# Graph stack, first attention layer: output sums divided by row sums before they are turned, the inverse taken through DRAM

## The chip, the cores and the metric

One core of one Trainium2 chip runs the whole program. The metric is device time in microseconds (us), lower is better. TensorE is called PE here, VectorE DVE, ScalarE ACT, GpSimd POOL and SyncE SP; PEld is PE's weight load. An engine works through its instructions in program order, so an instruction that waits holds up those behind it; SP computes nothing here and only issues DMAs.

## What is computed

Four layers on 4096 nodes with 256 features, each of the form `x = layernorm(x + layer(x, adj))`. The change touches the first layer alone, a graph attention with four heads of 64 features:

```
Wh = (h @ W).reshape(n, heads, d)
s_i = einsum('nhd,hd->nh', Wh, a[:, :d]);  s_j = einsum('nhd,hd->nh', Wh, a[:, d:])
e = leaky_relu(s_i[:, None, :] + s_j[None, :, :], 0.2)
e = where((adj == 0)[:, :, None], -inf, e)
alpha = softmax(e, axis=1)
out = einsum('ijh,jhd->ihd', alpha, Wh).reshape(n, heads * d)
return elu(out)
```

The softmax's division is done last: for each node and head a weighted sum of 64 features and one row sum are added up, and the sum is divided by the row sum.

## The kernel before

The first layer is `additive_heads`. The 4096 target nodes are cut into NB = 8 blocks b of QW = 512, the source nodes into NT = 32 tiles j of P = 128. For each (b, j):

- SP loads the mask, two tiles j at a time (L306), into one of four buffers ("mask", 512 KB).
- ACT makes the factors of one tile from `row` and `dst`, four instructions of 128x512 (L313; L311 in the tiles called APART, j = 3, 11, 19, 27), into one of seven buffers ("prob").
- DVE masks them: one instruction of 128x2048 (L328), in APART tiles four of 128x512 (L319).
- PE adds them up in `sums` (L338): for each of the four heads two matmuls for the 64 features and, outside APART, one for the row sum, into `acc[b]`, three PSUM banks: two with features, the third with row sums. The weights are 32 columns wide, and a head's results lie in its own 32 partitions. In the trace each such matmul is two records. In APART tiles POOL's DMA (L323, L325) collects the probabilities in `den` in place of the third matmul, and at the block's end four matmuls over `den` (L342) close the row sums.

PE stands in the order of the code, two units behind the weights (LAG = 2); in all other engines' streams a scheduler places the instructions. `masked`, `factors` and the like are handles of instructions, and `issue_after(handle)` orders an instruction behind another of the same engine without a semaphore.

When block b is summed, ACT copies one bank and DVE two of them to SBUF (`kept`, L346), and the block is finished in pieces while block b+1 runs (`finish`, called with the j of block b+1):

- j = 4 and 10: `turned` (L353): two groups of nodes at a time, three transposes each (two of features, one of row sums) into a PSUM bank "g". At j = 4, `rows(b + 2)` also puts one transpose of source terms (L292) into such a bank; ACT copies it to `line` (L294), SP writes it to DRAM in four DMAs ("far", L297) and reads it back to all partitions ("row", L299, 1 MB).
- j = 4, 7, 10, 13: `outputs` for one group each: reciprocal of four row sums per node (L358), division (L360), and the positive part of the result added to X (L232).
- j = 11, 14, 17, 20: `add_exponential` for one group each: ACT's exponential (L238), its part below 1 added to X on DVE (L239), and the statistics of the layernorm (L156, L157).
- j = 22 to 30: the root of variance plus EPS (L182 on DVE, L161 and L162 on ACT, L168 to L171 on DVE) and the scaling of the four groups (L186).

The last block (b = 7) is finished in `tail`, in the opening of the second layer. The pools that matter: "ga_z" (prob) 7 buffers, "ga_mask" 4, "ga_ps" (banks "g") 2, "ga_pa" (acc) 2, "ga_o" (the tile `o`) 4.

Of the kernel before, what the change touches and what calls it, by code (L numbers as in the profile page):

```python
# [9 lines left out]
FP = mybir.dt.float32  # L10
# [3 lines left out]
AF = mybir.ActivationFunctionType  # L14
OP = mybir.AluOpType
# [13 lines left out]
def kernel(  # L29
# [32 lines left out]
    def pool(stack, name, bufs, **kw):  # L62
        return stack.enter_context(tc.tile_pool(name=name, bufs=bufs, reuse_waits="tile", **kw))
# [5 lines left out]

    ident = const.tile([P, P], FP, name="ident")  # L70
    make_identity(nc, ident)
    ones = const.tile([P, P], FP, name="ones")
    nc.vector.memset(ones, 1.0)

# [21 lines left out]
    def spread(pl, ap, dims, shape, name, eng):  # L96

        sb = pl.tile(shape, FP, name=name)
        eng.dma_start(sb, bass.AP(tensor=ap.tensor, offset=ap.offset, ap=[[0, P]] + dims))
        return sb  # L100
# [53 lines left out]
    def one_row(mv, k, y):  # L154
        st = fin.tile([P, 6], FP, name="bn")
        nc.vector.bn_stats(st, y)  # L156
        nc.vector.bn_aggr(mv[:, k, :], st)  # L157
# [7 lines left out]
    def end_root(v, r, n, eng=nc.vector):  # L165

        s = fin.tile([P, n], FP, name=f"s{n}")
        eng.tensor_tensor(s, r, r, OP.mult)  # L168
        eng.tensor_tensor(s, s, v, OP.mult)
        eng.tensor_scalar(s, s, -0.5, 1.5, OP.mult, OP.add)  # L170
        eng.tensor_tensor(r, r, s, OP.mult)  # L171
# [7 lines left out]
    def begin_root(mv):  # L179
        n = mv.shape[1]  # L180
        v = fin.tile([P, n], FP, name=f"v{n}")
        nc.vector.tensor_scalar_add(v, mv[:, :, 1], EPS)  # L182
        return v, first_root(v, n), n

    def scale_row(y, mv, r, k):
        nc.vector.tensor_scalar(y, y, mv[:, k, 0:1], r[:, k:k + 1], OP.subtract, OP.mult)  # L186

# [46 lines left out]
    def add_exponential(o, b, k, mv, seen=None):  # L234

        y = X[:, b * QB + k, :D]
        with tc.issue_after(getattr(seen, "ins", seen)) if seen is not None else nullcontext():
            nc.scalar.activation(o, o, AF.Exp)  # L238
        nc.vector.scalar_tensor_tensor(y, o, 1.0, y, OP.min, OP.add)  # L239
        one_row(mv, k, y)  # L240

    def additive_heads(a, H, slope, early, narrow, ahead):
# [9 lines left out]
        with ExitStack() as lay:  # L252
# [10 lines left out]
            rp = pool(lay, "ga_row", 2)  # L263
            zp = pool(lay, "ga_z", 7)
            sb = pool(lay, "ga_sb", 2)
            op = pool(lay, "ga_o", 4)
            mp = pool(lay, "ga_mask", 4)
            dp = pool(lay, "ga_den", 1)
            dr = pool(lay, "ga_dram", 2, space=bass.MemoryType.DRAM)
# [5 lines left out]
            def bank():  # L275
                return ps.tile([P, QW], FP, name="g")
# [13 lines left out]
            def rows(b, pr):  # L290

                nc.tensor.transpose(pr[:QB * H, :P], src[:, b * QB:(b + 1) * QB, :].rearrange("p k h -> p (k h)"), ident)  # L292
                line = sb.tile([QB * H, P], FP, name="line")
                nc.scalar.copy(line, pr[:QB * H, :P])  # L294
                far = dr.tile([H, QB, P], FP, name="far")
                for k in range(QB):
                    nc.sync.dma_start(far[:, k, :], line[k * H:(k + 1) * H, :])  # L297
                row[b] = rp.tile([P, H, QW], FP, name="row")
                nc.sync.dma_start(row[b].rearrange("p h i -> p (h i)"),  # L299
                                  far.rearrange("h k i -> (h k i)").unsqueeze(0).to_broadcast([P, H * QW]))  # L300

            def weights(b, j, rows=None):
                m = b, j // MJ
                if j % MJ == 0:
                    mask[m] = mp.tile([P, MJ, QW], I32, name="mask")
                    nc.sync.dma_start(mask[m], edges[:, j:j + MJ, b * QW:(b + 1) * QW])  # L306
                z = prob[b, j] = zp.tile([P, H, QW], FP, name="prob")
                for h in range(H):
                    r = rows[h] if rows else row[b][:, h, :]
                    if j in APART:  # L310
                        seen = nc.scalar.mul(z[:, h, :], r, dst[:, j, h:h + 1])  # L311
                    else:
                        seen = nc.scalar.activation(z[:, h, :], r, AF.Relu, bias=-1.0, scale=dst[:, j, h:h + 1])  # L313
                factors[b, j] = seen
                if rows:
                    keep_rows(rows)
                if j in APART:
                    for h in range(H):
                        nc.vector.scalar_tensor_tensor(z[:, h, :], z[:, h, :], V[:, j, D + h:D + h + 1],  # L319
                                                       mask[m][:, j % MJ, :], OP.max, OP.mult)  # L320
                    if j == APART[0]:
                        den[b] = dp.tile([P, H, QW], FP, name="den")
                        seen = nc.gpsimd.dma_start(den[b], z)  # L323
                    else:
                        seen = nc.gpsimd.dma_start(den[b], z, accum_op=OP.add)  # L325
                    narrow(seen)
                    return
                nc.vector.scalar_tensor_tensor(z, z, 1.0, mask[m][:, j % MJ, :].unsqueeze(1).to_broadcast([P, H, QW]),  # L328
                                               OP.add, OP.mult)

            def sums(b, j):
                if j == 0:
                    acc[b] = pa.tile([P, HC + 1, QW], FP, name="acc")
                for n in range(HC if j in APART else HC + 1):
                    for h in range(H):
                        lo = h * d + n * G
                        part = V[:, j, lo:lo + G] if n < HC else V[:, j, D + h:D + h + 1].to_broadcast([P, G])
                        nc.tensor.matmul(acc[b][h * G:(h + 1) * G, n, :], part, prob[b, j][:, h, :],  # L338
                                         start=(j == 0), stop=(j == NT - 1 and n < HC))
                if j == NT - 1:  # L340
                    for h in range(H):
                        nc.tensor.matmul(acc[b][h * G:(h + 1) * G, HC, :], ones[:, :G], den[b][:, h, :],  # L342
                                         start=False, stop=True)
                    kept[b] = [fin1.tile([P, QW], FP, name=f"kept{c}") for c in range(HC + 1)]
                    for c in range(HC + 1):
                        (nc.vector.tensor_copy if c else nc.scalar.copy)(kept[b][c], acc[b][:, c, :])  # L346
                    mvs[b] = fin.tile([P, QB, 2], FP, name="mv")

            def turned(bank, b, k):

                po = bank().rearrange("p (c f) -> p c f", f=P)
                for c in range(HC + 1):
                    nc.tensor.transpose(po[:, c, :], kept[b][c][:, k * P:(k + 1) * P], ident)  # L353
                return po

            def outputs(sb, po, b, k):
                rden = fin.tile([P, H], FP, name="rden")
                nc.vector.reciprocal(rden, po[:, HC, ::G])  # L358
                o = out[b, k] = sb.tile([P, D], FP, name="o")
                nc.vector.tensor_tensor(o.rearrange("p (h c e) -> p h c e", h=H, c=HC),  # L360
                                        po[:, :HC, :].rearrange("p c (h e) -> p h c e", h=H),
                                        rden.unsqueeze(2).unsqueeze(3).to_broadcast([P, H, HC, G]), OP.mult)
                add_positive(o, b, k)

            def finish(b, j):

                if j in (4, 10):
                    k = (j - 4) // 3
                    pos[b, k], pos[b, k + 1] = turned(bank, b, k), turned(bank, b, k + 1)
                    if k == 0 and b + 2 < NB:  # L370
                        rows(b + 2, pos[b, 0][:, HC + 1, :])
                if j in (4, 7, 10, 13):
                    k = (j - 4) // 3
                    outputs(op, pos[b, k], b, k)
                if j in (11, 14, 17, 20):
                    k = (j - 11) // 3
                    add_exponential(out[b, k], b, k, mvs[b], factors[b + 1, j + LAG])
                elif j == 22:
                    roots[b] = begin_root(mvs[b])
                elif j == 24:  # L380
                    end_root(*roots[b])
                elif j in (25, 27, 28, 30):
                    k = (25, 27, 28, 30).index(j)
                    scale_row(X[:, b * QB + k, :D], mvs[b], roots[b][1], k)

            def turn(b, bank=bank):
                if b + 2 < NB:
# [6 lines left out]
                groups = [(0, HC + 1, side), (HC + 1, 1, bank().rearrange("p (n f) -> p n f", n=1))]  # L394
                additive_values(xTs[b], b, groups, w_sb, V, src, dst, H, slope, APART)

            pos, roots, xTs, out, factors = {}, {}, {}, {}, {}
            LAG = 2
            units = [(b, j) for b in range(NB) for j in range(NT)]
            with tc.manual_schedule(engines={mybir.EngineType.PE}):  # L400
# [1057 lines left out]
```

## Time and profile before

| | |
|---|---|
| median of 3 runs | 2767.89 us (2765.59 to 2771.09) |
| the profiled execution's own time | 2767.82 us |
| its span | 2766.0 us |
| PE busy over the span | 2750.1 us (99%) |
| DVE | 2311.0 us (84%) |
| ACT | 1696.6 us (61%) |
| POOL | 1075.5 us (39%) |
| granted PE clock in 100 to 700 us | 1.00 |

The profile is of one execution; its span starts with the first instruction and ends with the last. The first layer's sums run from about 20 us to 703 us. A line of a timeline gives start, duration, engine, source line, operation, output and inputs, and how many instructions were put together; in brackets stands the idle time of the engine before it and what ended it. Durations of neighbours overlap a little, so the distance from start to start is what one costs. "L338" is line 338 of the kernel before.

### The profile page before, as it was taken

How to read it: one execution, taken by the hardware profiler on the slowest of the kernel's cores; microseconds unless marked ns; L12 is line 12 of the kernel's file. 1: busy time of each engine (PE TensorE's matmuls, PEld its weight loads, DVE VectorE, ACT ScalarE, POOL GpSimd, SP SyncE). 2: the span in 40 equal slices, each digit the busy share in tenths (PEclk: the TensorE clock that was granted, in tenths of full speed). 3: DMA queues.
4: the chain of work that ended last, by engine and by line, in shares of the span. 5: the costliest groups of instructions: out<-in, count | busy, mean ns of one | idle time of the engine just before them, and what ended most of it. 6: DMA issues, size and time to landing. Idle time of an engine off the chain costs nothing. (4 is left out here: it accounts for less than half of the span.)

```text
span 2766.0 us, 50161 instructions
## 1 busy us (share of the span) xinstructions
PE 2750.1 (99%) x19365; PEld 1444.9 (52%) x19365; DVE 2311.0 (84%) x3121; ACT 1696.6 (61%) x2660; POOL 1075.5 (39%) x1020
## 2 busy tenths in 40 slices
PE   9999999999999999999999999999999999999999
PEld 5333333333543333333333336888888777777776
DVE  8899999999777788887888888888888876677776
ACT  8899999999346666666666665565655422222222
POOL 0000000000049878878788786454455000000000
PEclk9999999999999999999999999999999999999999
DMA  8798998987449899898998988577778544454442
GB/s 236 150 191 189 194 196 191 189 188 168 97 117 191 180 190 187 189 190 183 194 187 186 193 178 208 155 203 212 190 197 236 108 76 76 77 81 80 76 70 45
DMA packets 279673, 445.48 MB, mean 161 GB/s; under 512 B 55321, under 2 KB 156169, under 8 KB 274442
## 3 DMA queue, kind: packets, MB, share of 16 engines
q0 software_dynamic: 108784, 216.29, 46.9%
q1 hardware_dynamic: 164280, 218.88, 26.8%
q10 hardware_dynamic: 6370, 7.10, 0.8%
q8 instruction: 152, 2.49, 0.4%
q14 instruction: 87, 0.71, 0.1%
HBM read 335.94 MB, written 39.40 MB: 136 GB/s over the span
## 5 line engine op out<-in xcount | busy, mean ns | idle before, releaser
L888 DVE TENSOR_TENSOR prob<-p,mask 128x1024 f32<-128x1024 f32 x512 | 619.3, 1222 | 162.7 <-ACT p L878 157.0
L878 ACT ACTIVATE p<-p,shift 128x1024 f32<-128x1024 f32 x512 | 555.6, 1088 | 319.7 <-PE p L876 319.1
L338 PE MATMUL acc<-prob,V 128*32 128x512 f32 x5888 | 638.1, 593 | 1.2 <-DVE prob L328 1.1
L898 POOL TENSOR_TENSOR den<-den,prob 128x1024 f32<-128x1024 f32 x220 | 557.6, 2534 | 89.8 <-DVE prob L888 87.1
L313 ACT ACTIVATE prob<-row,dst 128x512 f32<-128x512 f32 x892 | 557.9, 711 | 3.3 <-PE acc L338 2.8
L876 PE MATMUL p<-qT,kT 64*64 64x512 f32 x4096 | 531.5, 591 | 2.3 <-DVE prob L888 2.3
L912 PE MATMUL acc<-prob,V 64*64 64x512 f32 x4096 | 530.1, 589 | 0.0
L328 DVE SCALAR_TENSOR_TENSOR prob<-prob,mask 128x2048 f32<-128x2048 f32 x224 | 507.4, 2285 | 12.6 <-ACT prob L313 11.7
L338 PEld LDWEIGHTS acc<-prob,V 128*32 128x32 f32 x5888 | 189.1, 110 | 434.1 <-issue 407.2
L484 PE MATMUL acc<-mix,mixed 128*128 128x256 f32 x1476 | 401.4, 380 | 1.9 <-DVE quarters L506 1.0
L912 PEld LDWEIGHTS acc<-prob,V 64*64 64x64 f32 x4096 | 157.6, 133 | 281.9 <-issue 280.1
L484 PEld LDWEIGHTS acc<-mix,mixed 128*128 128x128 f32 x1476 | 279.1, 190 | 45.3 <-PE acc L484 3.1
L876 PEld LDWEIGHTS p<-qT,kT 64*64 64x64 f32 x4096 | 154.4, 133 | 279.3 <-issue 252.1
L1185 DVE TENSOR_TENSOR prob<-prob,mask 128x1024 f32<-128x1024 f32 x128 | 156.4, 1222 | 142.9 <-ACT prob L1176 142.9
L904 POOL DMA_DIRECT2D den<-prob x240 | 233.5, 973 | 63.7 <-DMA den<-prob 34.1
L484 PE MATMUL acc<-prob,X 128*128 128x256 f32 x984 | 252.9, 380 | 0.6 <-ACT quarters L498 0.6
L1104 POOL DMA_DIRECT2D mask<-in_adjT x64 | 47.6, 744 | 529.1 <-DVE prob L1185 510.3
L484 PEld LDWEIGHTS acc<-prob,X 128*128 128x128 f32 x984 | 186.8, 190 | 79.8 <-issue 59.2
L617 DVE SCALAR_TENSOR_TENSOR prob<-r,own,mask 128x512 f32<-128x512 f32 x252 | 177.0, 743 | 48.1 <-POOL mix L476 11.9
L1176 ACT ACTIVATE prob<-p 128x512 f32<-128x512 f32 x144 | 86.1, 598 | 212.5 <-PE p L1172 212.5
L325 POOL DMA_DIRECT2D den<-prob x24 | 21.1, 878 | 475.7 <-DVE prob L319 475.7
L1176 ACT ACTIVATE prob<-g 128x512 f32<-128x512 f32 x112 | 66.9, 597 | 199.3 <-PE g L1172 199.3
(245 smaller groups left out, 3044.7 us busy)
## 6 DMA issues: line engine op xcount, KB each, us to landing
mask<-in_adjT SPq DMA_DIRECT2D x254, 512.0 KB
den<-prob POOLq DMA_DIRECT2D x240, 512.0 KB, 5.4
den<-prob POOLq DMA_DIRECT2D x32, 1024.0 KB, 9.2
mask<-edges SPq DMA_DIRECT2D x512, 64.0 KB
mask<-in_adjT POOLq DMA_DIRECT2D x64, 512.0 KB, 5.7
edges<-in_adj POOLq DMA_DIRECT2D x32, 512.0 KB, 17.1
far<-squares SPq DMA_DIRECT2D x16, 512.0 KB
den<-prob SPq DMA_DIRECT2D x16, 512.0 KB
```

Of the source, the lines that this page charges most:

```text
L313: seen = nc.scalar.activation(z[:, h, :], r, AF.Relu, bias=-1.0, scale=dst[:, j, h:h + 1])
L328: nc.vector.scalar_tensor_tensor(z, z, 1.0, mask[m][:, j % MJ, :].unsqueeze(1).to_broadcast([P, H, QW]), OP.add, OP.mult)
L338: nc.tensor.matmul(acc[b][h * G:(h + 1) * G, n, :], part, prob[b, j][:, h, :], start=(j == 0), stop=(j == NT - 1 and n < HC))
L484: nc.tensor.matmul(acc[at][:, half * HW:(half + 1) * HW], w, a, start=(g == 0 and n in (0, 2, 3, 5)), stop=(g == NP - 1), skip_group_check ...
L617: nc.vector.scalar_tensor_tensor(z[:, n, :], r, ga.own[:, j:j + 1], mask[:, n, :], OP.add, OP.mult)
L876: nc.tensor.matmul(p[c * d:(c + 1) * d, r, :], kT[half, c, at:at + d], qT[half, c, cols], start=True, stop=True)
L878: nc.scalar.activation(p, p, AF.Exp, bias=shift)
L888: nc.vector.tensor_tensor(z, p, mask[m][:, j % MJ, :].unsqueeze(1).to_broadcast([P, KC, QW]), OP.mult)
L898: nc.gpsimd.tensor_tensor(to, to, flat, OP.add)
L904: nc.gpsimd.dma_start(to, flat, accum_op=OP.add)
L912: nc.tensor.matmul(acc[b][c][r * d:(r + 1) * d, :], V[half, j, r * d:(r + 1) * d], prob[b, j][half, r, :], start=(j == 0), stop=(j == NH - 1))
L1185: nc.vector.tensor_tensor(z, z, co.mask[b, 2 * g // MJ][:, lo:lo + 2, :], OP.mult)
```

## The change

In the changed kernel, for the blocks 0 to 6, the features are divided while nodes still lie along the free axis, and turned afterwards:

- Only the row sums are copied at the end of a block, by ACT. Seven DMAs on SP's queue and one instruction make their inverse: `there` (four rows of 512 to DRAM), `few` (back as 128 x 16, so that a reciprocal costs 16 elements per partition), a reciprocal on DVE bound behind the masking of tile 9 of block b+1, `back` (to DRAM), and `rden` (four DMAs, each one row spread to 32 partitions).
- DVE multiplies the two feature banks in PSUM by `rden`, bound behind the masking of tile 14 of block b+1, in place of the copies. `acc[b]` is held until then.
- PE turns two groups at a time, at j = 14 and 16, with four transposes each and no row sums; the transposes write their bank in four runs of 32 columns. The transpose of `rows` stays at j = 4, alone, in a bank of its own.
- Positive part and exponential work on two groups in one instruction (128 x 512) and read PSUM.
- The mask load of tile 16 is ordered behind the last `rden` DMA on SP.
- The root takes EPS as ACT's bias, from a constant tile that POOL sets, and three DVE instructions replace five.
- "ga_o" has one buffer of each of its tiles in place of four.

For block 7 the three copies stay: ACT now makes two of them and DVE one. In the order of the built programs the engines' streams behind the first layer are the same.

```diff
+    eps = const.tile([P, 1], FP, name="eps")
+    nc.gpsimd.memset(eps, EPS)
...
+    def root_of(mv):
+        n = mv.shape[1]
+        r = fin.tile([P, n], FP, name=f"r{n}")
+        nc.scalar.activation(r, mv[:, :, 1], AF.Ln, bias=eps)
+        nc.scalar.activation(r, r, AF.Exp, scale=-0.5)
+        return r
+
+    def finish_root(r, var):
+
+        s = fin.tile(list(r.shape), FP, name=f"s{r.shape[1]}")
+        nc.vector.scalar_tensor_tensor(s, r, -0.5, r, OP.mult, OP.mult)
+        nc.vector.scalar_tensor_tensor(s, var, EPS, s, OP.add, OP.mult)
+        nc.vector.scalar_tensor_tensor(r, s, 1.5, r, OP.add, OP.mult)
...
-            op = pool(lay, "ga_o", 4)
+            op = pool(lay, "ga_o", 1)
...
-                    nc.sync.dma_start(mask[m], edges[:, j:j + MJ, b * QW:(b + 1) * QW])
+                    with after(spreads[b, j]) if (b, j) in spreads else nullcontext():
+                        nc.sync.dma_start(mask[m], edges[:, j:j + MJ, b * QW:(b + 1) * QW])
...
-                    kept[b] = [fin1.tile([P, QW], FP, name=f"kept{c}") for c in range(HC + 1)]
-                    for c in range(HC + 1):
-                        (nc.vector.tensor_copy if c else nc.scalar.copy)(kept[b][c], acc[b][:, c, :])
+                    total = fin1.tile([P, QW], FP, name=f"kept{HC}")
+                    nc.scalar.copy(total, acc[b][:, HC, :])
+                    if b < NB - 1:
+                        divided[b] = inverse_sums(b, total)
+                        next(divided[b])
+                    else:
+                        kept[b] = [fin1.tile([P, QW], FP, name=f"kept{c}") for c in range(HC)] + [total]
+                        for c in range(HC):
+                            (nc.vector.tensor_copy if c else nc.scalar.copy)(kept[b][c], acc[b][:, c, :])
...
+            def inverse_sums(b, total):
+
+
+                few = op.tile([P, H * QW // P], FP, name="few")
+                there, back = (dr.tile([H, QW], FP, name=name) for name in ("there", "back"))
+                spread = lambda t: t.rearrange("h (q r) -> (h q) r", r=H * QW // P)
+                nc.sync.dma_start(there, total.rearrange("(h g) i -> h g i", h=H)[:, 0, :])
+                nc.sync.dma_start(few, spread(there))
+                yield
+                with after(masked[b + 1, 9]):
+                    nc.vector.reciprocal(few, few)
+                nc.sync.dma_start(spread(back), few)
+                rdens[b] = op.tile([P, QW], FP, name="rden")
+                for h in range(H):
+                    seen = nc.sync.dma_start(rdens[b][h * G:(h + 1) * G, :], back[h:h + 1, :].to_broadcast([G, QW]))
+                spreads[b + 1, 16] = seen
+                yield
+                kept[b] = [fin1.tile([P, QW], FP, name=f"kept{c}") for c in range(HC)]
+                with after(masked[b + 1, 14]):
+                    for c in range(HC):
+                        nc.vector.tensor_tensor(kept[b][c], acc[b][:, c, :], rdens[b], OP.mult)
+                yield
...
+            def turned_pair(bank, b, k):
+
+                po = bank().rearrange("p (k f) -> p k f", f=D)
+                for n in range(2):
+                    for c in range(HC):
+                        nc.tensor.transpose(po[:, n, :].rearrange("p (h c g) -> p c h g", h=H, c=HC)[:, c],
+                                            kept[b][c][:, (k + n) * P:(k + n + 1) * P], ident)
+                return po
+
+            def pair_exponential(po, b, k, seen):
+
+                y = X[:, b * QB + k:b * QB + k + 2, :D]
+                e = op.tile([P, 2, D], FP, name="e")
+                with after(seen):
+                    nc.scalar.activation(e, po, AF.Exp)
+                nc.vector.scalar_tensor_tensor(y, e, 1.0, y, OP.min, OP.add)
+                for n in range(2):
+                    one_row(mvs[b], k + n, y[:, n, :])
...
+                if j == 4 and b + 2 < NB:
+                    rows(b + 2, bank())
+                elif j in (7, 13):
+                    next(divided[b])
+                elif j in (14, 16):
+                    k = j - 14
+                    po = pos[b, k] = turned_pair(bank, b, k)
+                    y = X[:, b * QB + k:b * QB + k + 2, :D]
+                    nc.vector.scalar_tensor_tensor(y, po, 0.0, y, OP.max, OP.add)
+                elif j in (21, 23):
+                    k = j - 21
+                    pair_exponential(pos[b, k], b, k, factors[b + 1, j + LAG])
+                elif j == 26:
+                    with after(factors[b + 1, 28]):
+                        roots[b] = root_of(mvs[b])
+                elif j == 28:
+                    finish_root(roots[b], mvs[b][:, :, 1])
+                if j >= 28:
+                    k = j - 28
+                    scale_row(X[:, b * QB + k, :D], mvs[b], roots[b], k)
```

## The prediction

> **What bounds the kernel now.** I read the busy time by stretches first, one stretch per block, cut at the starts of L342; its columns are busy time (and instructions) of PE, PEld, DVE, ACT and POOL, then PE's clock and the DMA share.
>
> ```profile
> 128.34:210.16 81.82, 81.82 (x762) 25.36 (x758) 80.55 (x80) 79.84 (x134) 6.40 (x8) 1.00 0.90 193
> 373.80:455.62 81.82, 81.82 (x762) 25.36 (x758) 80.96 (x79) 79.47 (x135) 6.41 (x8) 1.00 0.89 189
> 537.44:619.26 81.82, 81.82 (x762) 25.36 (x757) 81.06 (x79) 79.45 (x136) 6.41 (x8) 1.00 0.89 191
> ```
>
> PE, DVE and ACT are all nearly full. Every block takes exactly 81.82 us on PE, but an engine that is busy all the time need not be the one that sets the pace, so the timelines of PE and DVE come next, for block 4.
>
> ```profile
> 386.79 0.88 PE L353 MATMUL g<-ident,kept 128*128 128x128 f32 x6
> 387.50 0.27 PE L292 MATMUL g<-ident,src 128*16 128x128 f32 x1
> 387.70 15.66 PE L338 MATMUL acc<-prob,V 128*32 128x512 f32 x144
> 403.29 0.88 PE L353 MATMUL g<-ident,kept 128*128 128x128 f32 x6
> 404.09 51.71 PE L338 MATMUL acc<-prob,V 128*32 128x512 f32 x480
> 455.62 1.04 PE L342 MATMUL acc<-den,ones 128*32 128x512 f32 x8
> ```
>
> ```profile
> 380.59 1.28 DVE L346 COPY kept<-acc 128x512 f32<-128x512 f32 x2
> 393.33 0.24 DVE L358 RECIPROCAL rden<-g 128x4 f32<-128x4 f32 x2
> 394.88 2.73 DVE L319 SCALAR_TENSOR_TENSOR prob<-prob,V,mask 128x512 f32<-128x512 f32 x4
> 401.94 0.42 DVE L239 SCALAR_TENSOR_TENSOR X<-o,X 128x256 f32<-128x256 f32 x1
> 463.56 1.28 DVE L346 COPY kept<-acc 128x512 f32<-128x512 f32 x2
> ```
>
> PE's records run at one steady pace: 480 in 455.62 - 404.09 = 51.53 us, 0.1074 us each. DVE's period, from L346 to L346, is 463.56 - 380.59 = **82.97 us**, 1.15 us longer than PE's. Both can be true because DVE starts ahead and loses its lead. Tile 11 (APART, L319) shows it: here DVE ends it at 397.61, PE starts it at 404.09, a lead of 6.5 us. The same two events in blocks 1 and 7:
>
> ```profile
> 145.98 2.73 DVE L319 SCALAR_TENSOR_TENSOR prob<-prob,V,mask 128x512 f32<-128x512 f32 x4
> ...
> 644.36 2.08 DVE L319 SCALAR_TENSOR_TENSOR prob<-prob,V,mask 128x512 f32<-128x512 f32 x3
> ```
>
> PE starts that tile at 158.63 in block 1 (lead 158.63 - 148.71 = 9.9 us) and at 649.45 in block 7 (3.0 us). So PE sets the first layer's time from 103 us on, and DVE uses up a store that just lasts. Only PEld's timeline near the layer's end shows it empty; and ACT's shows what stretches the other loop:
>
> ```profile
> 697.27 0.16 PEld L338 LDWEIGHTS acc<-prob,V 128*32 128x32 f32 x8 [0.93 <-DVE prob L328]
> ...
> 705.61 1.96 PE L786 MATMUL g<-xT,wk_sb 128*128 128x512 f32 x4 [0.20 <-DVE kept L346]
> ```
>
> ```profile
> 431.60 0.20 ACT L161 ACTIVATE r<-v 128x4 f32<-128x4 f32 x1 [2.35 <-DVE v L182]
> ```
>
> Usual idle time between weight loads is 0.30, so PE loses some 0.6 us to DVE in the whole layer.
>
> The Trainium skill (Perfetto Trace Analysis, Identifying the Most-Contended Engine) warns that matmul busy time misleads and asks for weight-load time instead. PEld is 25.36 of 81.82 here, 31%, which by that rule makes DVE with 99% the engine to relieve; the sum would then be the second rival's below. The steady 0.1074 us and the lead speak against it: 32-column weights load in little time, and matmuls are still back to back.
>
> **The change part by part.**
>
> *PE.* The price of an insertion comes from gaps. Six transposes (L353): from 404.09 back to 387.70 are 16.39 us, less 144 records at 0.1074 = 15.46, leaves 0.93. With L292: 12.20 us of sums start at 374.66 with 112 records (12.02), so 386.68 to 387.70 is 1.02. Eight transposes (L117, one place in block 7): 184 records start at 649.45, end by pace at 669.20, sums go on at 670.35: 1.15. Two transposes more cost 0.22, so one costs 0.11, switching 0.28, L292 0.09. Before: 1.02 + 0.93 = 1.95 per block. After: L292 alone 0.37, two insertions of four 0.28 + 0.43 = 0.71 each, 1.79. That is 0.15 less in blocks 1 to 6, 0.9 in all; block 7 has no L292, 1.86 becomes 1.43, 0.4. **PE: -1.3 us.** One thing is not in the trace: the new transposes write four runs of 32 columns. Between no cost and twice the time of 56 transposes (+6.0) I take none: 32-column and 128-column outputs both run at PE's pace here.
>
> *DVE*, start to start. Gone: two L346 1.20; two groups of L358, L360, L232 (393.33 to 394.88, 1.55) 3.10; four L239 at 0.34, 1.36; the five small root steps about 0.8; sum 6.5. Added: a reciprocal of 16 elements about 0.1 (L358's four take 0.12), two multiplications of 128x512 from PSUM at L346's 0.60, two positive parts and two additions of the same width, 3.6 in all; three small steps 0.4; sum 4.1. Statistics and scaling stay, later. **DVE's loop loses 2.4 us per block**, 82.97 becomes 80.6, shorter than PE's 81.67. This is off the path: it ends the draining and is worth only the 0.6 us near the layer's end.
>
> *ACT.* Four L238 at 0.31 become two of 128x512 at 0.47 (L346 on ACT), -0.3, and the wait of 2.35 in front of L161 goes: the new logarithm stands before tile 29, the last statistics it needs before DVE's tile 27. The new exponentials read a bank filled after PE's tile 14 or 16, in front of ACT's tiles 24 and 26. Nothing on the path: 0.
>
> *End of the layer.* In block 7 PE's first product of the second layer pauses at 705.58, where its pace asked for 704.81, until DVE's second copy has ended at 705.46. With two copies on ACT and one on DVE the banks are free by 704.7 to 705.3: -0.2 to -0.77, I take **-0.4**.
>
> *SP's queue.* Seven DMAs per block more. `there` waits for ACT's copy, which ACT reaches before tile 6, `few` for `there`, `back` for the reciprocal, `rden` for `back`; behind them on SP stand `rows`' DMAs and the mask of tile 16. Nearest rows are those of L297 and L299:
>
> ```profile
> 391.87 1.28 SPq L297 DMA_DIRECT2D far<-line  x4
> 395.33 0.35 SPq L299 DMA_DIRECT2D row<-far  x1
> 397.65 0.39 SPq L306 DMA_DIRECT2D mask<-in_adjT  x1
> ```
>
> A round through DRAM holds SP for 395.33 - 393.15 = 2.2 us after the last issue. From the reciprocal: issue 0.3, `back` 2.2, three `rden` 0.9, L299 behind its own wait some 1 to 1.5, the fourth `rden` 0.3, and L299's 1 MB ahead of it in the queue (3.3 us at the queue's 65.42 MB in 34.3% of 600 us; 6 if POOL's accumulation runs at once), landing 2.2: **10.5 to 13.5 us**. Cover: DVE masks tiles 10 to 14 meanwhile, four at 2.21 and one APART at 2.66, 11.5 us. So DVE may wait 0 to 2 us before the first multiplication, less than its gain of 2.4 per block, while a lead near 10 us stands behind it. PE needs the multiplied features only after its tile 14, over 6 us behind DVE's. The mask of tile 16 goes out about 7 us after the reciprocal, in place of at once, and is needed 13 us after it. I take 0 on the path; below nothing is excluded, since no DMA goes away. [...]
>
> Sum: -1.3 - 0.6 - 0.4 = **-2.3 us**. Against the profiled execution's 2767.82 that is 2765.5; the median shown, 2767.89, is the same to 0.1. Behind the layer all engines have the same order, and PE is full there, so the shift should pass through.
>
> **Rivals.**
>
> *The inverse comes late (slower).* If the way from the reciprocal to `rden` takes C, DVE stands C - 11.5 us per block. Free are 81.67 - 80.6 = 1.1 us per block and a lead of 9.9: PE loses 7 x (C - 12.6) - 9.9, more than nothing from C = 14.0 on, 2.5 us above DVE's cover. At C = 16 that is +13.9, with the gains 2779. For it: DMA share 0.89 to 0.92, POOL's 1 MB accumulation takes a median of 9.2 us, 16 elements per row make small packets. Against it: mask loads never held DVE in this stage, and L299 comes through quickly.
>
> *DVE is the true bound (faster).* If the occupancy is right, 2.4 x 7 = 17 us go: 2751. Against it: PE's steady pace; only 0.6 us of waits.
>
> *Turning costs more.* Strided outputs or longer switching: up to +6 on my sum, 2771.5, most likely half.
>
> **How the numbers follow.** My own case 0.75 (2763 to 2768), late inverse 0.13, DVE bound 0.05, dearer turning 0.07. About 0.2%, 5.5 us, is what a measurement of this kernel can tell from no change; runs of it already lie 5.5 us apart. Faster by more: DVE bound and a corner of my case, 0.07. Slower by more: the late inverse, and little of the dear turning, 0.14. Within: 0.79. The range takes my case, dear turning and the first part of a late inverse: 2761 to 2773.
>
> **What would show it.** In the changed profile: PE's block period near 81.67; DVE's lead at tile 11 staying near 10 us up to block 7; a wait of DVE before the first multiplication of at most 2 to 3 us, named after the DMA; no idle time over 0.3 us of PEld on DVE near the end of the layer. I am wrong if the lead shrinks in spite of DVE's lighter loop, if DVE waits on masks at tile 16, or if an insertion of four transposes takes over 1 us.

## The result and the profile after

The changed kernel takes 2776.36 us (median of 8 runs, 2774.70 to 2781.71), the kernel before 2768.78 in the 8 runs beside it: a ratio of 1.003, with an interval of 1.0019 to 1.0041, or **7.6 us slower**. The profiled execution took 2774.97 us, its span is 2773.0.

All the loss lies in one place. This is PE's timeline of the changed kernel, with the products that close blocks 6 and 7 (L359, before L342) and block 7 from its first turned pair (L403) on; L355 are the sums, L119 (before L117) is `ahead`, the eight transposes that prepare the second layer's first block.

```profile
617.18 1.04 PE L359 MATMUL acc<-den,ones 128*32 128x512 f32 x8
...
655.07 0.66 PE L403 MATMUL g<-ident,kept 128*128 128x128 f32 x4
655.65 5.36 PE L355 MATMUL acc<-prob,V 128*32 128x512 f32 x48
...
661.52 5.36 PE L355 MATMUL acc<-prob,V 128*32 128x512 f32 x48
669.91 1.12 PE L119 MATMUL g<-ident,X 128*128 128x128 f32 x4 [3.03 <-ACT e L412]
675.29 1.12 PE L119 MATMUL g<-ident,X 128*128 128x128 f32 x4 [4.26 <-ACT e L412]
676.34 33.84 PE L355 MATMUL acc<-prob,V 128*32 128x512 f32 x296
710.00 1.03 PE L359 MATMUL acc<-den,ones 128*32 128x512 f32 x8
```

Blocks 1 to 5 take 81.61 to 81.62 us each, as hoped for; block 6 takes 81.86; block 7 takes 710.00 - 617.18 = **92.82 us**, 9.63 more than the 702.45 - 619.26 = 83.19 before. The kernel before has `ahead` (L117) at the same unit, without a wait, and closes block 7 with L342:

```profile
669.33 1.09 PE L117 MATMUL g<-ident,X 128*128 128x128 f32 x8
...
702.45 1.04 PE L342 MATMUL acc<-den,ones 128*32 128x512 f32 x8
```

In the changed kernel's brackets PE stands still twice, each time until an exponential of ACT (L412) has read one of the two banks "g". ACT's timeline has the same two moments: they are in the row of the factors, where the order of the program puts them, ahead of tiles 24 and 26.

```profile
669.28 0.57 ACT L412 ACTIVATE e<-g 128x512 f32<-128x512 f32 x1
...
674.66 0.58 ACT L412 ACTIVATE e<-g 128x512 f32<-128x512 f32 x1
```

They end at 669.85 and 675.24, and PE's transposes start at 669.91 and 675.29. There is a second loss behind the first. In the busy time by stretches (columns as in the prediction, the granted clock in front of the DMA share) PE's clock falls to one half as the first wait ends (0.99 is still the mean of 666 to 670) and stays there through the second wait and after PE has work again:

```profile
670.00:674.00 4.00, 1.03 (x4) 0.63 (x4) 3.97 (x7) 4.00 (x7) 0.00 (x0) 0.50 1.02 166
...
678.00:682.00 4.00, 4.00 (x32) 1.07 (x28) 3.72 (x8) 1.95 (x4) 0.00 (x0) 0.73 0.38 67
```

The price from the timeline: the 48 records from 661.52 end by pace at 666.68, and sums go on at 676.34, 9.66 us later, where by the same measure eight transposes cost 1.13 (e1 below: 160 records from 619.62 end by pace at 636.80, sums go on at 637.93): 8.5 lost. The 296 records after it take 710.00 - 676.34 = 33.66, at the usual pace 296 x 0.1074 = 31.79: 1.9 lost to the clock. Together 10.4.

**Off the path**, the rest did not go as forecast either. DVE is busy less (392.97 us of the 408 from 128 to 536, before 403.38), but its lead over PE shrank all the same. Measured at tile 10 of blocks 1 to 7 (end of masking to the start of PE's sums):

| | b1 | b2 | b3 | b4 | b5 | b6 | b7 |
|---|---|---|---|---|---|---|---|
| before | 10.6 | 9.5 | 8.3 | 7.2 | 6.0 | 4.9 | 3.6 |
| after | 9.6 | 8.6 | 7.0 | 6.1 | 4.7 | 4.9 | 2.3 |

DVE's waits in the changed kernel, 127 to 710 us (total, times, longest), the longest of ACT's, and one of DVE's for a mask, in block 3:

```profile
DVE prob L345 <- ACT prob L330: 10.0, 13, 3.3
DVE prob L345 <- DMA mask<-in_adjT: 5.4, 2, 2.8
...
DVE kept L392 <- DMA rden<-back: 0.2, 1, 0.2
```

```profile
ACT prob L330 <- DMA den<-prob: 9.4, 7, 2.3
```

```profile
324.84 6.70 DVE L345 SCALAR_TENSOR_TENSOR prob<-prob,mask 128x2048 f32<-128x2048 f32 x3 [2.55 <-DMA mask<-in_adjT]
```

The inverse itself is in time (0.2 us in all). Two other things are late. DVE waits 10.0 us for ACT's factors, before 4.2, and ACT itself stands 9.4 us until POOL's DMA into `den` has given a buffer "prob" back, which it never did before. And tile 16's mask is late, for which SP's queue of the same block shows a cause: the mask stands behind the last `rden`, and so also behind the 1 MB of `row` (L315), which `rows` reads back.

```profile
307.33 0.34 SPq L383 DMA_DIRECT2D back<-few  x1
...
310.42 1.23 SPq L386 DMA_DIRECT2D rden<-back  x3
311.82 0.34 SPq L315 DMA_DIRECT2D row<-far  x1
312.20 0.43 SPq L386 DMA_DIRECT2D rden<-back  x1
312.68 31.92 SPq L323 DMA_DIRECT2D mask<-in_adjT  x8
```

The mask goes out at 312.68 and DVE gets it at 324.84, 12.2 us later; DVE was free for it at 324.84 - 2.55 = 322.29, 9.6 us after the issue.

### The profile page after: what moved, and what is told of

The parts are those of the page before. It is cut to its first block, busy times and chain, and to the rows that moved or that the text cites. A ratio compares the mean times of both kernels' runs of the same rounds, so it can differ in the third digit from the quotient of the medians.

```text
span 2773.0 us, 50094 instructions
## 1 busy us (share of the span) xinstructions
PE 2750.0 (99%) x19337; PEld 1439.2 (52%) x19337; DVE 2294.8 (83%) x3029; ACT 1696.8 (61%) x2647; POOL 1075.7 (39%) x1021
## 5 line engine op out<-in xcount | busy, mean ns | idle before, releaser
L355 PE MATMUL acc<-prob,V 128*32 128x512 f32 x5888 | 641.1, 594 | 1.2 <-DVE prob L345 1.2
L355 PEld LDWEIGHTS acc<-prob,V 128*32 128x32 f32 x5888 | 188.0, 110 | 433.4 <-issue 410.8
L342 POOL DMA_DIRECT2D den<-prob x24 | 21.1, 878 | 474.3 <-DVE prob L336 474.3
```

## The experiments

**Theory:** `ahead` at unit 20 of block 7 needs both banks "g", and the change now holds both from PE's turning behind tiles 14 and 16 until ACT's exponentials ahead of tiles 24 and 26. In the kernel before, the second bank was free after DVE's divisions (L360, 658.45 to 659.21), and `ahead` started at 669.33 without a wait. **Rivals:** the late inverse of the prediction, directly or through DVE's shrinking lead; and a loss by the clock alone. A second question is what ate DVE's gain. The kernel before, run beside them, took 2771.05 us (15 runs) for e1, e3, e4, e5, 2768.41 (33) for e6 to e9 and 2768.30 (21) for e10 and e12.

### The two banks

**e1**, `ahead` earlier, when the banks are free:

```diff
-                    if i == (NB - 1) * NT + 20:
+                    if i == (NB - 1) * NT + 8:
```

> Changed kernel with one line moved: the transposes of the second layer's first block (ahead, L119) at unit 8 of block 7 in place of unit 20, when both banks g are free. Theory BANKS: the whole loss is PE waiting in block 7 for the two banks that the turned pairs hold until their exponentials (8.6 us of idle time), plus about 2 us in which the granted clock is halved after it; so about 10 us go, and the kernel stands 1 to 3 us below the kernel before (block 7 takes 82 to 84 us on PE). Theory LEAD: PE waits because DVE and ACT have lost their lead by block 7; then the wait turns up later in block 7 and at most 3 us go.

Measured: 2770.59 us, 0.9996 (0.9988 to 1.0005). Block 7 takes 82.44, the clock stays at 1.00, and `ahead` takes 637.93 - 636.90 = 1.03 us from its start to the next sums. The whole loss is gone; whether the kernel is below the one before, as expected, the interval doesn't tell. DVE's lead at tile 10 still falls, to 2.8 in block 6, so the lead was not what made the loss.

**e5**, the same collision in the kernel *before*, which has none of the inverse's DMAs:

```diff
-                    if i == (NB - 1) * NT + 20:
+                    if i == (NB - 1) * NT + 12:
```

> Kernel before with ahead at unit 12 in place of unit 20, two units after both banks g were taken by the turned groups 2 and 3; nothing of the division or of DRAM is in it. BANKS: PE waits for the outputs of those groups, which stand before DVE's tile 17; 3 to 8 us slower than the kernel before. LEAD: DVE has its lead of 2 to 3 us there as before, and no new wait on DRAM: within 1 us.

Measured: 2781.53 us, 1.0037 (1.0025 to 1.005), +10.5 us, more than expected. PE's timeline of this kernel:

```profile
658.19 1.94 PE L117 MATMUL g<-ident,X 128*128 128x128 f32 x8 [9.50 <-DVE o L360]
```

One wait of 9.5 us, then transposes at 1.94 in place of 1.09 at half the clock. So the same loss comes without the change, if `ahead` meets banks in use. The late inverse is out as its cause.

**e6**, the changed kernel with no instruction moved, only with `ahead`'s transposes in a free buffer of the sums' pool:

```diff
-                        ahead(bank)
+                        spare = pa.tile([P, HC + 1, QW], FP, name="acc")
+                        free = iter([spare[:, 0, :], spare[:, 1, :]])
+                        ahead(lambda: next(free))
```

> Changed kernel with ahead where it was, at unit 20 of block 7, but its eight transposes write the banks of the free acc tile (block 6's, empty since its features were multiplied) in place of banks g. BANKS: the wait at L119 is gone without any instruction moved, block 7 takes 82 to 83 us on PE, and the kernel stands within 3 us of the one with ahead at unit 8, 8 to 10 below the changed kernel. If the wait had to do with the place (DVE or ACT late there), 5 us and more remain.

Measured: 2767.22 us, 0.9993 (0.9984 to 1.0002); block 7 takes 82.43, 10.4 less than in the changed kernel. This is the cleanest proof of the banks: the exponentials are where they were in the program. It also shows the second loss: blocks 4 to 6 take 82.25, 82.67 and 82.42, where 81.62 is PE's own. DVE waits 11.0 us for masks here (four times, 4.4 at the longest) and 6.4 for ACT, which waits 10.1 for `den`; DVE's lead is down to 0.1 at tile 26 of block 4, and PE loses some 2.5 us. How much of it is chance is open: up to block 6 the changed kernel, e1, e7 and e8 have the same program and lost 0.25, 0.57, 0.40 and 0.69 us there, each in one profiled execution.

**e8**, `ahead` at unit 22, nearer to the second exponential:

```diff
-                    if i == (NB - 1) * NT + 20:
+                    if i == (NB - 1) * NT + 22:
```

> Changed kernel with ahead at unit 22 in place of 20, about 5 us later on PE. BANKS: the first bank is free by then (ACT's first exponential ended at 669.9), the second one not quite (675.2): a wait of 1.5 to 3 us is left, and if so short a wait leaves the clock at 1.00, block 7 takes 84 to 85.5 us on PE and the kernel is 1.5 to 3 us slower than with unit 8. If the clock halves all the same, 2 us more.

Measured: 2769.78 us, 1.0005 (0.9996 to 1.0014); the first bank is free, one wait is left, a little longer than expected, and block 7 takes 87.69, over the 84 to 85.5 expected. The expectation that the clock stays up in so short a wait failed: it is halved for 3.41 us, from 677.0 on, after PE had gone on.

```profile
675.71 0.65 PE L119 MATMUL g<-ident,X 128*128 128x128 f32 x4 [3.34 <-ACT e L412]
```

**e7**, the changed kernel with 19 products of a constant ahead of each of `ahead`'s two groups, into a free buffer that nobody reads, so that PE is busy while it waits:

```diff
+            if busy:
+                busy(BUSY)
...
+                        def busy(n):
+                            for _ in range(n):
+                                nc.tensor.matmul(spare[:, 0, :P], ones, ones, start=True, stop=True)
```

> Changed kernel with 19 idle products of 128x128 on the free acc tile before each of ahead's two groups of four transposes, some 4 us each, so that PE works where it stood still; nothing else is computed with them. If the halved clock of 10.24 us after the stall is a separate price, the clock stays at 1.00 and block 7 on PE is 1.5 to 2.5 us shorter than the changed kernel's 92.8, or the same plus what the idle products are too long by; if the stall alone costs the time, the idle products save nothing (0 or worse).

Measured: 2773.26 us, 1.0016 (1.0007 to 1.0025). The banks are as late as before, the clock stays at 1.00, and the 296 records after it take 31.97 in place of 33.84:

```profile
676.76 31.97 PE L358 MATMUL acc<-prob,V 128*32 128x512 f32 x296
```

Block 7 takes 90.99, 1.83 less than 92.82. So of the 10.4 us some 8.6 are the banks and 1.8 the clock that follows.

### SP's queue

**e3**, the mask of tile 16 not ordered behind `rden` any more:

```diff
-                    with after(spreads[b, j]) if (b, j) in spreads else nullcontext():
-                        nc.sync.dma_start(mask[m], edges[:, j:j + MJ, b * QW:(b + 1) * QW])
+                    nc.sync.dma_start(mask[m], edges[:, j:j + MJ, b * QW:(b + 1) * QW])
```

> Changed kernel without the binding of tile 16's mask behind the rden DMAs (ahead stays at unit 20). BANKS: no change beyond 1 us of the changed kernel, about 7 us above the kernel before; the wait at L119 stays between 7 and 9 us. LEAD: DVE no longer waits for the mask at tile 16 (2.6 us in blocks 3 and 4), keeps a lead near 10 us, and over half of the loss goes.

Measured: 2799.30 us, 1.0097 (1.0081 to 1.0112). Neither theory had that; the wait for the banks stays, 7.5 us. SP's queue in block 3: a mask that waits for a buffer now stands between `back` and `rden`, and `row`'s 1 MB ahead of all four.

```profile
316.34 0.35 SPq L382 DMA_DIRECT2D back<-few  x1
319.97 0.39 SPq L322 DMA_DIRECT2D mask<-in_adjT  x1
320.54 0.33 SPq L315 DMA_DIRECT2D row<-far  x1
320.96 2.17 SPq L385 DMA_DIRECT2D rden<-back  x4
```

The waits of this kernel show the rival of the prediction at work, and PE behind it:

```profile
DVE kept L391 <- DMA rden<-back: 32.6, 6, 6.1
...
PE g L402 <- DVE kept L391: 12.8, 9, 3.6
```

By the two ratios, 1.0097 against 1.003, the ordering of the mask is worth about 19 us: with `row` where it stands, the inverse is in time only because of it.

**e4**, e1's and e3's edits together.

> Both edits: ahead at unit 8 and the mask of tile 16 unbound. BANKS: as with ahead moved alone, less up to 1 us that PE lost to DVE at the end of blocks 6 and 7; 2 to 3 us below the kernel before. LEAD: the sum of both single gains, and only here the loss is gone. DVE's lead over PE at tile 11 of block 7 should be 6 us or more, against 2 in the changed kernel.

Measured: 2790.52 us, 1.0064 (1.0051 to 1.0076), 8.8 us under e3, with 32.2 us of waits for `rden`; neither theory's time came true. The two effects add up: by the ratios the banks' price is 9.1 us beside the late inverse (e3 to e4) and 9.4 without (changed kernel to e1).

**e9**, e1 with the last `rden` ahead of the mask of tile 18, in place of 16:

```diff
-                spreads[b + 1, 16] = seen
+                spreads[b + 1, 18] = seen
```

> Kernel with ahead at unit 8, and the binding on the mask of tile 18 in place of tile 16, so that tile 16's mask is loaded ahead of the way through DRAM while no later mask gets between. If the mask of tile 16 takes DVE's gain, DVE has no wait on masks, keeps a lead of over 5 us at tile 11 of block 7, and the time is that of the kernel with unit 8 or up to 1 us less. If the way to rden gets too long (L299's 1 MB now stands ahead of all four rden), DVE waits 1 to 5 us per block for rden, the lead is used up by block 4 or 5, and the time is 3 to 15 us above.

Measured: 2769.96 us, 1.0003 (0.9994 to 1.0013). No wait for a mask is left, but 17.5 us of waits for `rden`, which now comes behind `row` and the mask; the lead is down to 0.1 at its least in blocks 5 and 6, and block 6 takes 83.96. The time is that of e1 within the intervals, not 3 to 15 us above. To exchange mask and `rden` only moves the wait: the megabyte between them stays. That made `row` the suspect.

**e12**, e6 with `rows` five tiles later, the mask's order as in the changed kernel:

```diff
-                if j == 4 and b + 2 < NB:
+                if j == 9 and b + 2 < NB:
```

> The same with the binding left on the mask of tile 16: only rows' DMAs go behind rden. If L299's 1 MB ahead of that mask in the queue made it late, DVE's waits on masks fall under 1 us per block and the lead stays, as with the binding on tile 18. If the place behind the round through DRAM makes it late, waits of 2 to 4 us stay in several blocks, and the lead is used up by block 6 or 7.

Measured: 2764.94 us, **0.9986 (0.9977 to 0.9995)**. SP's queue in block 3 has nothing between `back` and `rden`, and `far` and `row` are behind the masks:

```profile
306.02 0.34 SPq L383 DMA_DIRECT2D back<-few  x1
308.13 2.55 SPq L386 DMA_DIRECT2D rden<-back  x4
310.72 4.96 SPq L323 DMA_DIRECT2D mask<-in_adjT  x3
317.76 1.97 SPq L313 DMA_DIRECT2D far<-line  x4
```

DVE waits for no mask and no `rden`, for ACT only 0.6 us at a time, and ACT for `den` 0.4 in all: both late things are gone with the one move of `rows`. What is left are 5.3 us of waits for `few`, ahead of the reciprocal. DVE's lead at tile 10 is 9.7, 9.0, 8.5, 8.9, 8.6, 9.0, 8.5 in blocks 1 to 7; it is held there by ACT, which waits for free buffers (15 waits for PE, 4.7 us in all). Blocks 1 to 6 take 81.62 each, block 7 82.44.

**e10**, e12 with e9's edit as well.

> Kernel with ahead in the spare banks, plus: rows of block b+2 at j = 9 in place of 4, so that L297's and L299's DMAs come behind rden on SP, and the binding on the mask of tile 18, so that tile 16's is loaded first. If DVE's gain of 2.4 us per block was lost to the order on SP's queue alone, DVE now waits neither for masks nor for rden (under 1 us per block), keeps a lead of over 6 us at tile 11 of block 7, PE takes 81.6 us in every one of blocks 1 to 6, and the time is 1 to 2 us under the kernel with the spare banks, some 2 to 3 under the kernel before. If the loop is held by something else (ACT, or the accumulation of den that holds a prob buffer), the lead shrinks by 0.5 to 1.5 us per block as before, and the time stays within 1 us of the kernel with the spare banks.

Measured: 2764.74 us, 0.9986 (0.9977 to 0.9995), one wait of 2.8 us for `rden`, lead 8.2 in block 7. With `row` out of the way it makes no difference which of the two goes first. e10 and e12 are the only versions that are clearly faster than the kernel before, by 3.4 to 3.6 us; by the ratios they are some 12 us under the changed one.

## Why the prediction was wrong

- **The step that failed: "*PE.* The price of an insertion comes from gaps."** `ahead` was read there as one more sample of what eight transposes cost, at "one place in block 7", and nowhere as a user of the banks "g". The term that was put at nothing is ACT's: "Nothing on the path: 0." The two facts that make the wait both stood in front of it: the new exponentials "read a bank filled after PE's tile 14 or 16, in front of ACT's tiles 24 and 26". They were counted as instructions and not as the time for which a bank is held, so that nobody asked who needs a bank in between. None of the rivals had it; the chance of 0.14 for a slower kernel was given to the late inverse and a dearer turning, and neither made this loss. Price: 8.6 + 1.8 us, shown by e1, e6, e7 and, in the kernel before, by e5.
- **PE's terms: right.** A block lost 0.20 us (forecast 0.15), an insertion of four transposes costs 661.52 - 655.65 = 5.87 less 48 records (5.16), 0.71 as forecast, so strided outputs cost nothing that shows. From the first closing product to the last, e12 takes 572.14 us against 574.11: 1.97 less, the forecast's 1.3 + 0.6. In e1, where DVE's lead still drains, it is 1.40.
- **End of the layer: right in mechanism, half in size.** The pause before the fifth product of the second layer is gone; the first eight take 714.78 - 710.96 = 3.82 us, before 3.99. 0.17, not 0.4.
- **"it ends the draining": wrong.** DVE's loop did get lighter: from 128 to 536 us it was busy for 403.38 us in 408 / 82.97 = 4.92 loops, 82.0 each, and in e12, whose loop keeps PE's 81.62, for 398.71 us in 5.00, 79.8 each; 2.3 us, of 2.4 worked out. But in the changed kernel waits took their place, and two of the prediction's own signs of being wrong came: the lead shrank in spite of the lighter loop, and DVE waited on masks at tile 16. The queue's "I take 0 on the path" failed for that mask: it went out 5.6 us after the reciprocal (forecast 7), but the time from the issue to the landing was left out, 12.2 us against 9.6 that there were. The 1 MB ahead of it had been counted for the last `rden` and not for the mask behind it. ACT's waits for `den`, 9.4 us, stood in no term. In the changed kernel all this costs PE little (block 6 lost 0.25). Its price alone isn't settled: 2.5 us in e6's blocks 4 to 6 and nothing in e12's, but 0.25 to 0.69 in the other executions, and the ratios, 0.9993 in e6 against 0.9986 in e12, lie within each other's intervals.
- **The late inverse: right to doubt it here.** From 307.05, the reciprocal, to the multiplication at 318.81 there are 11.8 us, and `rden` is there. But its chance hung on one line of the diff: without the mask's order it happens (e3). That the kernel came out slower, as this rival had it, is no point for it: the loss has another cause.
- **DVE as the true bound: refuted.** In e12 DVE is lighter, its lead stays at 8.5, and the block remains at 81.62.

What stays open: the layer and the transition account for 2.0 + 0.17 us of the 3.4 that e12 measures (interval 1.4 to 6.4); the rest of the program, the same in all these kernels, took 2060 to 2069 us in the profiled executions, so the remainder can't be told from chance. Exponentials moved ahead of tile 20 were not tried.

## What to carry to other kernels

When a change keeps a buffer longer, list every user of its pool over that time, the rare ones from other parts of the program too, and set the time of release beside the time of the next request. When an engine is made lighter, look at what it waits for next: if its loads share an in-order queue, order and size of what stands ahead decide whether the gain stays. A large transfer with slack should stand behind a small one without.

## What the hardware showed that was not expected

A wait of PE costs more than its length. In the changed kernel the granted clock is halved for 10.24 us from the end of the first wait on (669.92 to 680.16), and for the same 10.24 us from 653.44 on, inside the wait of 9.50, in e5; for 3.41 us, a third of that, behind a single wait of 3.34 in e8, where it begins 1.3 us after PE has gone on. With idle products in the wait (e7) it isn't halved at all. In e3 and e4 PE also waits for the late inverse, and the clock is halved for 3.41 us behind waits of 2.57 and 3.59 (e3) and of 1.89, 2.80 and 3.76 (e4), but not behind one of 2.94 (e3). So length alone doesn't decide.

The Trainium skill (TensorE: Matmul & The Clock Gate, Part 1: The HAM clock gate) has the clock at one half after an idle window of about 3.4 us, in a free-running window of 3413 ns. The lengths measured here are one, two (6.83 in e3's block 7) and three such windows, and in e4 the halvings begin 85.33 us apart, 25 windows, though the waits before them begin 87.5 and 85.7 apart. A whole idle window isn't needed: in e4 PE is busy for 1.31 of the 3.41 us from 418.87 to 422.28, and the next 3.41 us are at half. e3's wait of 2.94 falls on two windows, counted back from its own halvings, with 1.86 and 1.82 us of work, and the clock stays up. By the page's table one busy window ends the halving; in the changed kernel the clock stayed down for 680.16 - 675.29 = 4.9 us after the last wait (0.73 is the mean of 678 to 682): the window in which the work begins, 673.33 to 676.75, holds 1.45 us of it, and the next one is the first that PE fills.
